# Pauses in a dispatch, a reordered prologue and two moved pieces of work in a two-layer MoE and ternary FFN kernel

## The chip, the core and the metric

One core of a Trainium2 chip runs the whole program in one launch. Its engines work side by side: TensorE (PE) multiplies, VectorE (DVE) and ScalarE (ACT) work on elements, GpSimd (POOL) does the same and issues indirect transfers, SyncE (SP) issues the plain ones. Each engine takes its own instructions strictly in order. The metric is device time in microseconds (us), from the first instruction to the last; lower is better.

## What is computed

The input x has 128 x 32 tokens of 256 numbers, 4096 rows in all. Two layers are added to it in turn. Cut to what matters, with the router's sigmoid and the quantization's clips left in words:

```python
# layer 0: a linear layer with a low-rank adapter per batch, then a mixture of experts
h = x @ W.T + scalings[idx] * ((x @ A[idx].T) @ Bm[idx].T)
scores = sigmoid(h @ gate_w.T)                    # 8 experts, the 2 best of each token
routed = sum over the two: onehot(expert) * ((silu(s*h @ w1.T) * (s*h @ w3.T)) @ w2.T)
shared = (silu(h @ ws1.T) * (h @ ws3.T)) @ ws2.T
x = x + shared + routed
# layer 1: mixing of a batch's 32 rows by a gathered 32x32 matrix, then an FFN of ternary weights
y = einsum("bct,bcd->bdt", x, cond_weights[idx1])
u = act_quant(fwht(y)) @ weight_quant(w_up).T
x = x + act_quant(fwht(relu(u) ** 2)) @ weight_quant(w_down).T
```

`weight_quant` divides by the mean absolute weight, rounds to -1, 0 or 1 and scales back. `fwht` is a Walsh-Hadamard transform.

## The kernel before

The 4096 rows are 32 tiles of 128, taken in 8 groups (`NG`) of 4 tiles (`GT`). The program has four stages.

*Projection and routing* (lines 125 to 427, in a pool named `stage`). The host has laid out transposed copies. `project(g)` makes the adapter's inner product (pa, L214), then the layer's output and the router's logits together for each tile (ph, L226 and L229); ScalarE moves them to `hc[g]`. Eight columns of the router come from a small product of W and the gate (pt_gw, L187) that VectorE copies into `WT` and `BT` (L196, L197). `route(g)` is some twenty small VectorE instructions that rank the eight scores and count, so that each token's two rows have a place `dest` in the expert's region of the buffer `xs` in device memory. Then GpSimd issues eight indirect transfers for the group (L303), one for each tile and choice: 64 in all, called the dispatch here. Every row has its own place, so that they need not wait for each other.

*Around it*: loads of all inputs on SP's queue (L141 to L160), four small ones on ScalarE's; one indirect gather of the mixing matrices (wc, L162), first in GpSimd's queue behind some memsets, which goes through device memory (cs, L168) into the block-diagonal `bd` (L181); the ternary weights, made by VectorE from `ud` (L317 to L350); a table of slots (`slot_table`, L352 to L397), which says which expert each tile of 128 dispatched rows belongs to; and zeros behind each region (`pad`, L412, on SP).

*Shared expert and slots*. `shared_up` and `shared_down` run the shared expert group by group (pt_h L435, pgs L445, hids L452, pos L460), six groups (`SHARED1`) before the slots and two after them. In the slots, SP reads 128 dispatched rows (xin, L502), TensorE turns them over (pt_s, L510), VectorE or ScalarE evacuates (xTs, L84 or L86), then come the expert's two products (pg L536, po L562), and GpSimd scatters the results (yt, L569). A first read of xin waits until the dispatch has landed; 36 pairs of slots follow each other in a pipeline. VectorE's small work for a slot is cm, c and to (L519, L525, L526).

*Combination and layer 1* (L614 to the end): adds, the mixing, the transforms and the ternary products.

The order of work on each engine is that of a scheduler which goes by what is ready in its own model, except where a call asks for program order. Tiles are tracked for dependences. Plain transfers rotate over eight semaphores, so a load also waits until the load eight before it has landed; the indirect ones do the same over eight of their own. The body of `shared_up` and `shared_down` is not changed, only its place in the file.

Of the kernel before, what the change touches and what calls it, by code (L numbers as in the profile page):

```python
# [7 lines left out]
F32 = mybir.dt.float32  # L8
# [3 lines left out]
AF = mybir.ActivationFunctionType  # L12
ALU = mybir.AluOpType
AX = mybir.AxisListType

P = 128
D = 256
B, T = 128, 32
NT = B * T // P
GT = 4  # L20
NG = NT // GT
# [14 lines left out]
SHARED1 = 6  # L36


C_ID, C_H, C_HS, C_TRI, C_E16, C_N16 = 0, 128, 256, 640, 704, 712
# [5 lines left out]
def tile_kernel(  # L45
# [20 lines left out]
    nc = tc.nc  # L66
# [9 lines left out]
    def bank(tag, name, shape=(P, 512), dtype=F32):  # L76
        return psum.tile(list(shape), dtype, tag=tag, name=name)
# [3 lines left out]
    def evac(dst, src):  # L81
        turn[0] += 1
        if turn[0] % 2:
            nc.vector.tensor_copy(dst, src)  # L84
        else:
            nc.scalar.copy(dst, src)  # L86
# [25 lines left out]
    with tc.tile_pool(name="moe", bufs=1) as moe, tc.tile_pool(name="work1", bufs=2) as work1:  # L112
# [4 lines left out]
        ws2T = ws[:, 2 * D :]  # L117
# [4 lines left out]
        tab = moe.tile([P, 2, NSLOT], I32, name="tab")  # L122


        with tc.tile_pool(name="stage", bufs=1) as stage:
            wn = stage.tile([P, 2, D], F32, name="wn")
            bn = stage.tile([P, 2, P], F32, name="bn")
# [11 lines left out]

            nc.scalar.dma_start(GW, gate)  # L140
            nc.sync.dma_start(wn, W.rearrange("(c p) d -> p c d", p=P))  # L141
            nc.scalar.dma_start(i1, idx1.rearrange("(b o) -> b o", o=1))
            nc.sync.dma_start(AT, AT_)
            nc.sync.dma_start(xT[0], xT_[0])
            nc.scalar.dma_start(
                i0, idx0.rearrange("(o b) -> o b", o=1).partition_broadcast(P)
            )
            nc.scalar.dma_start(
                sb, scal.rearrange("(o e) -> o e", o=1).partition_broadcast(P)
            )  # L150
            nc.sync.dma_start(WT[:, :, :D], WT_)
            nc.sync.dma_start(bn, Bm)
            nc.sync.dma_start(cst, consts)
            nc.sync.dma_start(BT[:, :D], BT_)
            for g in range(1, NG):
                nc.sync.dma_start(xT[g], xT_[g])
            nc.sync.dma_start(ws, shared_)
            nc.sync.dma_start(wall[:, : E * WCOL // 2], experts[:, : E * WCOL // 2])
            nc.sync.dma_start(wall[:, E * WCOL // 2 :], experts[:, E * WCOL // 2 :])
            nc.sync.dma_start(ud, updown)  # L160

            nc.gpsimd.indirect_dma_start(  # L162
                out=wc,
                out_offset=None,
                in_=cw.rearrange("s c d -> s (c d)"),
                in_offset=bass.IndirectOffsetOnAxis(ap=i1, axis=0),
            )
            nc.sync.dma_start(cs, wc)  # L168

            zeros = stage.tile([P, ROW], F32, name="zeros")  # L170
            cnt = stage.tile([P, E], F32, name="cnt")
            nc.gpsimd.memset(zeros, 0.0)
            nc.gpsimd.memset(cum[:, 0], 0.0)
# [1 line left out]
            nc.gpsimd.memset(ones, 1.0)  # L175
            nc.gpsimd.memset(half, HALF)
            nc.gpsimd.memset(bd, 0.0)
            csv = cs.rearrange("(n q) (c d) -> q c n d", q=4, d=T)
            for q in range(4):
                s = slice(32 * q, 32 * q + 32)  # L180
                nc.sync.dma_start(bd[s, :, s], csv[q])  # L181


            pt = bank("t", "pt_gw")
# [21 lines left out]
                mask, i0, cst[:, C_N16 : C_N16 + 1], scol, ALU.is_equal, ALU.mult  # L206
            )
            nc.vector.tensor_copy(upper, cst[:, C_U : C_U + P])
            nc.vector.tensor_copy(idh, ident)

            def project(g):
                pa = bank("x", f"pa{g}")
# [19 lines left out]
            def route(g):  # L232
# [66 lines left out]
                nc.vector.tensor_copy(dest, df)  # L299

                for n in range(GT):
                    for i in range(2):
                        ins = nc.gpsimd.indirect_dma_start(  # L303
                            out=xs,
                            out_offset=bass.IndirectOffsetOnAxis(
                                ap=dest[:, i, n : n + 1], axis=0
                            ),
                            in_=hc[g][:, n],
                            in_offset=None,
                        ).ins  # L310
                        tc.declare_no_dep(ins, group="xs", reason="every pair has its own row")
                        tc.add_to_no_dep_group("xs", ins)

            def ternary_weights():
                rs = stage.tile([P, 2], F32, name="rs")
                part = stage.tile([P, 2, 16], F32, name="part")
                nc.vector.tensor_reduce(  # L317
                    part,
                    ud.rearrange("p i (a b) -> p i a b", a=16),
                    AX.X,  # L320
                    ALU.add,
                    apply_absolute_value=True,
                )
                nc.vector.tensor_reduce(rs, part, AX.X, ALU.add)
                pw = bank("x", "pw", (P, 2))
                nc.tensor.matmul(pw, ones, rs, start=True, stop=True)
                wscale = stage.tile([P, 2], F32, name="wscale")
                wrec = stage.tile([P, 2], F32, name="wrec")
                nc.vector.tensor_scalar(wscale, pw, 1.0 / (FF * D), EPS, ALU.mult, ALU.max)
                nc.vector.reciprocal(wrec, wscale)  # L330

                k0 = stage.tile([P, 1], F32, name="k0")
                nc.vector.scalar_tensor_tensor(
                    k0, wscale[:, 0:1], FF**-0.5, wscale[:, 0:1], ALU.mult, ALU.mult
                )
                k1 = stage.tile([P, 2], F32, name="k1")
                nc.vector.tensor_tensor(k1[:, 0:1], k0, wscale[:, 1:2], ALU.mult)
                nc.vector.reciprocal(k1[:, 1:2], k0)  # L340
                nc.vector.tensor_scalar(k1[:, 1:2], k1[:, 1:2], EPS / QB, None, ALU.mult)
                nc.vector.tensor_copy(kc, k1.unsqueeze(2).to_broadcast([P, 2, 2]))

                outs = [upT.rearrange("p k f -> p (k f)"), dnT.rearrange("p f d -> p (f d)")]
                for i in range(2):
                    nc.vector.tensor_scalar(
                        ud[:, i], ud[:, i], wrec[:, i : i + 1], MAGIC, ALU.mult, ALU.add
                    )
                    nc.vector.tensor_scalar(ud[:, i], ud[:, i], -MAGIC, 1.0, ALU.add, ALU.min)
                    nc.vector.tensor_scalar(outs[i], ud[:, i], -1.0, None, ALU.max)  # L350
# [62 lines left out]
                    tc.declare_no_dep(ins, group="xs", reason="no pair has a row of the padding")  # L413
                    tc.add_to_no_dep_group("xs", ins)

            xg = []
            for g in range(NG):
                project(g)
                if g > 0:
                    route(g - 1)  # L420
            for g in range(NG):
                xg.append(cpool.tile([P, GT, D], F32, tag="x", name=f"x{g}", bufs=NG))
                nc.sync.dma_start(xg[g], xt[g])
            route(NG - 1)
            slot_table()
            pad()
            ternary_weights()


        def shared_up(g):  # L430
            hT = work1.tile([P, 2, GT * P], F32, tag="hT", name=f"hT{g}")
            for k in range(2):
                pt = bank("t", f"pt_h{g}_{k}")
                for n in range(GT):
                    nc.tensor.transpose(  # L435
                        pt[:, n * P : (n + 1) * P],
                        hc[g][:, n, k * P : (k + 1) * P],
                        ident,
                    )
                evac(hT[:, k], pt)  # L440
            pgs = []
            for i in range(2):
                pg = bank("m", f"pgs{g}_{i}")
                for k in range(2):
                    nc.tensor.matmul(  # L445
                        pg, ws13[:, k, i], hT[:, k], start=(k == 0), stop=(k == 1)
                    )
                pgs.append(pg)
            sil = work1.tile([P, 512], F32, tag="xa", name=f"sils{g}", bufs=4)
            hid = work1.tile([P, 512], F32, tag="xa", name=f"hids{g}", bufs=4)  # L450
            nc.scalar.activation(sil, pgs[0], AF.Silu)
            nc.vector.tensor_tensor(hid, pgs[1], sil, ALU.mult)  # L452
            return hid

        def shared_down(g, hid):
            for h in range(2):
                po = bank("o", f"pos{g}_{h}", (P, 2, D))
                for i in range(2):
                    n = 2 * h + i
                    nc.tensor.matmul(  # L460
                        po[:, i], hid[:, n * P : (n + 1) * P], ws2T, start=True, stop=True
                    )
                v = xg[g][:, 2 * h : 2 * h + 2]
                nc.vector.tensor_tensor(v, po, v, ALU.add)

        def shared(gs):
            hid = None
            for g in [*gs, None]:
                nxt = shared_up(g) if g is not None else None
                if hid is not None:  # L470
                    shared_down(*hid)
                hid = (g, nxt)

        shared(range(0, SHARED1))

        tc.no_sync_barrier()

# [402 lines left out]
```

## Time and profile before

| | |
|---|---|
| median of 13 runs | 389.69 us (386.91 to 391.38) |
| the profiled execution: its own time / its span | 390.04 us / 388.2 us |
| granted TensorE clock, mean | 0.979 |
| busy: PE / DVE / ACT / POOL | 356.3 / 223.1 / 164.2 / 227.2 us |
| share of PE in the chain that ended last | 84% |
| dispatch, L303: busy, mean of one, number | 63.8 us, 997 ns, 64 |
| scatter, L569: busy, mean of one, number | 70.0 us, 973 ns, 72 |
| transfers: mean rate over the span | 148 GB/s |

The span runs from the first to the last instruction that the profiler recorded; the time of the execution has some 1.8 us around it. Busy time is an engine's time inside instructions. TensorE is busy for 92% of the span, so most of its time is work that cannot go away; the rest is where it waited, and whose wait ended last there.

In 40 equal slices of 9.7 us, the page shows TensorE's busy share in tenths, the clock granted to it, and the transfer engines' share:

```profile
PE   3999999918997999999999999999899999999983
...
POOL 5007777787740265554655655749887887745450
PEclk9999999977999999999999999999999999999996
DMA  7999846453236354444543422155333323001111
```

The ninth slice, from 78 to 87 us, has a digit of 1 for TensorE, with a lowered clock there and in the slice after it. GpSimd's digits from the fourth to the twelfth slice are the dispatch.

### The profile page before, as it was taken

Reading aid. Unit: us, or ns where it says so; the run is one execution under the profiler, and the core shown is the slowest. Engines: PE = TensorE matmul, PEld = TensorE weight load, DVE = VectorE, ACT = ScalarE, POOL = GpSimd, SP = SyncE. Lnnn points to the kernel's source line nnn. Section 1 sums busy time; section 2 is a strip of 40 time slices with the busy share of each in tenths; the row PEclk is TensorE's granted clock in tenths of the full one; section 3 lists DMA queues with packets and bytes.
Section 4 is the critical chain, followed back from the end, with each engine's and each line's share of the span. In section 5 each row is a group of like instructions: output and inputs, shape, how many; then the busy total and the mean of one; then the engine's idle time right before and its main releaser. Section 6 shows DMA issues by size and latency. Waiting matters only on the chain.

```text
span 388.2 us, 6544 instructions
## 1 busy us (share of the span) xinstructions
PE 356.3 (92%) x2055; PEld 281.2 (72%) x2055; DVE 223.1 (57%) x714; ACT 164.2 (42%) x328; POOL 227.2 (59%) x259
## 2 busy tenths in 40 slices
PE   3999999918997999999999999999899999999983
PEld 2667767604665788887787888657789898998771
DVE  0157867794355565554655555334667576676762
ACT  1021221401111444444343444315586877777862
POOL 5007777787740265554655655749887887745450
PEclk9999999977999999999999999999999999999996
DMA  7999846453236354444543422155333323001111
GB/s 214 408 427 340 251 165 214 166 206 109 106 117 202 107 163 134 151 165 141 171 158 122 160 81 76 54 201 182 109 109 130 115 83 104 34 29 57 54 56 54
DMA packets 38882, 57.49 MB, mean 148 GB/s; under 512 B 9278, under 2 KB 28736, under 8 KB 38465
## 3 DMA queue, kind: packets, MB, share of 16 engines
q1 hardware_dynamic: 31600, 39.17, 30.5%
q0 software_dynamic: 6672, 17.84, 12.5%
q10 hardware_dynamic: 576, 0.08, 0.3%
q8 instruction: 17, 0.28, 0.3%
q14 instruction: 17, 0.13, 0.1%
HBM read 33.93 MB, written 24.18 MB: 150 GB/s over the span
## 4 chain that ended last, share of the span: by engine, by line
PE 84%; DVE 6%; DMA 2%; issue 2%; ACT 2%; POOL 2%; SPq 1%; DVEq 0%; ACTq 0%
PE pg L536 17%; PE ph L226 8%; PE po L562 8%; PE pr L722 7%; PE pf L638 7%; PE pgs L445 7%; PE pa L214 4%; PE ph L229 4%; PE pt_s L510 4%; PE py L622 4%; PE pd L760 3%; PE pu L692 3%; PE pos L460 2%; PE phd L553 2%; PE pq L750 2%
## 5 line engine op out<-in xcount | busy, mean ns | idle before, releaser
L569 POOL DMA_INDIRECT yt<-y,to x72 | 70.0, 973 | 69.3 <-DVE cm L519 24.6
L303 POOL DMA_INDIRECT xs<-hc,dest x64 | 63.8, 997 | 42.7 <-DVE s L239 23.5
L536 PE MATMUL pg<-wall,xTs 128*128 x288 | 76.7, 390 | 3.1 <-DVE cm L519 2.2
L536 PEld LDWEIGHTS pg<-wall,xTs 128*128 128x128 f32 x288 | 49.2, 190 | 15.0 <-DVE hid L545 5.4
L544 ACT ACTIVATE sil<-pg,c 128x128 f32<-128x128 f32 x72 | 26.4, 367 | 58.4 <-PE pg L536 55.5
L545 DVE SCALAR_TENSOR_TENSOR hid<-pg,c,sil 128x128 f32<-128x128 f32 x72 | 25.1, 348 | 44.5 <-ACT sil L544 44.2
L614 POOL TENSOR_TENSOR x<-x,y 128x512 f32<-128x512 f32 x32 | 40.5, 1270 | 6.4 <-PE pgs L445 5.2
L562 PE MATMUL po<-wall,hidT 128*128 x144 | 37.7, 381 | 0.0
L638 PE MATMUL pf<-cst,yT 128*128 128x256 f32 x128 | 34.9, 394 | 1.6 <-ACT yT L630 1.6
L722 PE MATMUL pr<-cst,b 128*128 128x128 f32 x256 | 34.8, 280 | 1.2 <-POOL b L711 0.7
L226 PE MATMUL ph<-WT,xT 128*128 128x264 f32 x128 | 35.5, 404 | 0.3 <-DVE WT L196 0.3
L230 ACT COPY hc<-ph 128x264 f32<-128x264 f32 x32 | 12.1, 378 | 52.2 <-PE ph L229 45.4
L722 PEld LDWEIGHTS pr<-cst,b 128*128 128x128 f32 x256 | 31.0, 192 | 1.7 <-POOL b L711 0.9
L226 PEld LDWEIGHTS ph<-WT,xT 128*128 128x128 f32 x128 | 25.5, 200 | 7.9 <-issue 2.2
L445 PE MATMUL pgs<-hT,ws 128*128 128x512 f32 x64 | 30.4, 618 | 0.4 <-DVE hT L84 0.4
L562 PEld LDWEIGHTS po<-wall,hidT 128*128 128x128 f32 x144 | 24.5, 190 | 2.2 <-ACT hidT L86 0.3
L460 PE MATMUL pos<-ws,hids 128*128 128x256 f32 x64 | 16.8, 394 | 9.0 <-DVE hids L452 9.0
L638 PEld LDWEIGHTS pf<-cst,yT 128*128 128x128 f32 x128 | 21.5, 191 | 4.3 <-ACT yT L630 2.3
L510 PE MATMUL pt_s<-cst,xin 128*128 128x128 f32 x144 | 24.2, 273 | 0.0
L736 ACT ACTIVATE q<-pr,half,sc 128x512 f16<-128x512 f32 x32 | 23.1, 779 | 2.1 <-DVE sc L733 2.1
L710 POOL TENSOR_TENSOR b<-c 128x512 f32<-128x512 f32 x16 | 20.3, 1266 | 4.2 <-DVE m L729 2.7
L445 PEld LDWEIGHTS pgs<-hT,ws 128*128 128x128 f32 x64 | 12.2, 199 | 13.9 <-issue 11.3
(137 smaller groups left out, 639.6 us busy)
## 6 DMA issues: line engine op xcount, KB each, us to landing
xin<-xs SPq DMA_DIRECT2D x72, 136.0 KB, 2.3
y<-yt SPq DMA_DIRECT2D x16, 512.0 KB, 3.7
xT<-in_xT SPq DMA_DIRECT2D x8, 512.0 KB, 8.5
x<-in_x SPq DMA_DIRECT2D x8, 512.0 KB, 4.5
out<-o SPq DMA_DIRECT2D x16, 256.0 KB, 2.1
wall<-in_experts SPq DMA_DIRECT2D x2, 1536.0 KB, 12.3
yt<-y,to POOLq DMA_INDIRECT x72, 2.6
xs<-zeros SPq DMA_DIRECT2D x8, 136.0 KB, 2.1
```

Of the source, the lines that this page charges most:

```text
L226: nc.tensor.matmul(ph, xT[g][:, k, cols], WT[:, k], start=(k == 0), stop=False)
L303: ins = nc.gpsimd.indirect_dma_start(out=xs, out_offset=bass.IndirectOffsetOnAxis(ap=dest[:, i, n : n + 1], axis=0), in_=hc[g][:, n], in_o ...
L445: nc.tensor.matmul(pg, ws13[:, k, i], hT[:, k], start=(k == 0), stop=(k == 1))
L510: nc.tensor.transpose(pt[:, i, k], xin[:, i, k * P : (k + 1) * P], ident)
L536: nc.tensor.matmul(pg[:, i].rearrange("p a f -> p (a f)"), xT[:, i, k], wall[:, bass.ds(w + k * D, D)], start=(k == 0), stop=(k == 1),)
L544: nc.scalar.activation(sil[:, i], pg[:, i, 0], AF.Silu, scale=ci)
L545: nc.vector.scalar_tensor_tensor(hid[:, i], pg[:, i, 1], ci, sil[:, i], ALU.mult, ALU.mult)
L562: nc.tensor.matmul(po[:, i], hT[:, i], wall[:, bass.ds(w + 2 * D, D)], start=True, stop=True)
L569: ins = nc.gpsimd.indirect_dma_start(out=yt, out_offset=bass.IndirectOffsetOnAxis(ap=to[:, i : i + 1], axis=0), in_=y[:, i], in_offset=Non ...
L614: nc.gpsimd.tensor_tensor(v, v, y2[:, :, r], ALU.add)
L638: nc.tensor.matmul(pf[:, i], yT[:, k, i * P : (i + 1) * P], had256[k], start=(k == 0), stop=(k == 1),)
L722: nc.tensor.matmul(pr[:, f * P : (f + 1) * P], b[:, f, i * P : (i + 1) * P], had, start=True, stop=True,)
```

## The change

Four things are edited.

1. *A pause for every eight dispatch transfers*: after each group's transfers but the last, GpSimd fills a tile `pause` of 128 x 1600 numbers that nobody reads, and the next group's transfers are issued after it.
2. *Loads in order*: `bn` goes ahead of `AT` and `xT[0]`, the constants are loaded in two parts, the second (identity and transforms) after `xT[4]`, and i1 goes last on ScalarE's queue. The f16 copy of the identity (idh) moves from the front of VectorE's work to behind the routing.
3. *The mixes' gather*, with its way through device memory into `bd`, becomes a function called after the third `project`, so that its place in GpSimd's queue is after the second pause, and cs and bd come later in SP's queue, behind four of the eight x loads.
4. *The ternary weights* are made inside the shared expert: `shared` takes a function `amid` and calls it after the third group's step. The shared functions move up in the file for that, and the call of `shared` goes inside the pool `stage`.

```diff
+            for i, g in enumerate([*gs, None]):
+                nxt = shared_up(g) if g is not None else None
+                if hid is not None:
+                    shared_down(*hid)
+                hid = (g, nxt)
+                if i == 2 and amid is not None:
+                    amid()
...
             nc.scalar.dma_start(GW, gate)
             nc.sync.dma_start(wn, W.rearrange("(c p) d -> p c d", p=P))
-            nc.scalar.dma_start(i1, idx1.rearrange("(b o) -> b o", o=1))
-            nc.sync.dma_start(AT, AT_)
-            nc.sync.dma_start(xT[0], xT_[0])
             nc.scalar.dma_start(
                 i0, idx0.rearrange("(o b) -> o b", o=1).partition_broadcast(P)
             )
+            nc.sync.dma_start(bn, Bm)
...
+            nc.sync.dma_start(AT, AT_)
+            nc.sync.dma_start(xT[0], xT_[0])
+            nc.scalar.dma_start(i1, idx1.rearrange("(b o) -> b o", o=1))
             nc.sync.dma_start(WT[:, :, :D], WT_)
-            nc.sync.dma_start(bn, Bm)
-            nc.sync.dma_start(cst, consts)
+            nc.sync.dma_start(cst[:, C_TRI:], consts[:, C_TRI:])
             nc.sync.dma_start(BT[:, :D], BT_)
             for g in range(1, NG):
                 nc.sync.dma_start(xT[g], xT_[g])
+                if g == 4:
+                    nc.sync.dma_start(cst[:, :C_TRI], consts[:, :C_TRI])
...
-            nc.gpsimd.indirect_dma_start(
-                out=wc,
-                out_offset=None,
-                in_=cw.rearrange("s c d -> s (c d)"),
-                in_offset=bass.IndirectOffsetOnAxis(ap=i1, axis=0),
-            )
-            nc.sync.dma_start(cs, wc)
...
+            pause = stage.tile([P, 1600], F32, name="pause")
...
-            nc.vector.tensor_copy(idh, ident)
...
                 for n in range(GT):
-                    for i in range(2):
-                        ins = nc.gpsimd.indirect_dma_start(
...
+                    with ExitStack() as stack:
+                        if paused:
+                            stack.enter_context(tc.issue_after(paused[-1].ins))
+                        for i in range(2):
+                            ins = nc.gpsimd.indirect_dma_start(
...
+                    if n == GT - 1 and g < NG - 1:
+
+                        paused.append(tc.keep_in_program_order(nc.gpsimd.memset(pause, 0.0)))
+
+            paused = []
...
+            def mixes():
+
+                tc.keep_in_program_order(
+                    nc.gpsimd.indirect_dma_start(
+                        out=wc,
...
+                nc.sync.dma_start(cs, wc)
+                csv = cs.rearrange("(n q) (c d) -> q c n d", q=4, d=T)
+                for q in range(4):
+                    rows = slice(32 * q, 32 * q + 32)
+                    nc.sync.dma_start(bd[rows, :, rows], csv[q])
+
             for g in range(NG):
                 project(g)
                 if g > 0:
                     route(g - 1)
+                if g == 2:
+                    mixes()
...
             route(NG - 1)
+            tc.keep_in_program_order(nc.vector.tensor_copy(idh, ident))
             slot_table()
             pad()
-            ternary_weights()
...
-        shared(range(0, SHARED1))
+            shared(range(0, SHARED1), ternary_weights)
```

More of the change, by code (lines that the diff above doesn't have):

```diff
@@ L122, in tile_kernel, with shared_up, shared_down, shared @@
         tab = moe.tile([P, 2, NSLOT], I32, name="tab")
+        xg = []
+        def shared_up(g):
+            hT = work1.tile([P, 2, GT * P], F32, tag="hT", name=f"hT{g}")
+            for k in range(2):
+                pt = bank("t", f"pt_h{g}_{k}")
+                for n in range(GT):
+                    nc.tensor.transpose(
+                        pt[:, n * P : (n + 1) * P],
+                        hc[g][:, n, k * P : (k + 1) * P],
+                        ident,
+                    )
+                evac(hT[:, k], pt)
+            pgs = []
+            for i in range(2):
+                pg = bank("m", f"pgs{g}_{i}")
+                for k in range(2):
+                    nc.tensor.matmul(
+                        pg, ws13[:, k, i], hT[:, k], start=(k == 0), stop=(k == 1)
+                    )
+                pgs.append(pg)
+            sil = work1.tile([P, 512], F32, tag="xa", name=f"sils{g}", bufs=4)
+            hid = work1.tile([P, 512], F32, tag="xa", name=f"hids{g}", bufs=4)
+            nc.scalar.activation(sil, pgs[0], AF.Silu)
+            nc.vector.tensor_tensor(hid, pgs[1], sil, ALU.mult)
+            return hid
+        def shared_down(g, hid):
+            for h in range(2):
+                po = bank("o", f"pos{g}_{h}", (P, 2, D))
+                for i in range(2):
+                    n = 2 * h + i
+                    nc.tensor.matmul(
+                        po[:, i], hid[:, n * P : (n + 1) * P], ws2T, start=True, stop=True
+                    )
+                v = xg[g][:, 2 * h : 2 * h + 2]
+                nc.vector.tensor_tensor(v, po, v, ALU.add)
+        def shared(gs, amid=None):
+            hid = None
+            for i, g in enumerate([*gs, None]):
[5 more added lines that the diff above has]
+                    amid()
         with tc.tile_pool(name="stage", bufs=1) as stage:
@@ L177, in tile_kernel @@
             nc.gpsimd.memset(bd, 0.0)
[L178 to L181, printed above, removed]
             pt = bank("t", "pt_gw")
@@ L301, in route @@
                 for n in range(GT):
-                    for i in range(2):
[L303 to L312, printed above, removed]
+                    with ExitStack() as stack:
+                        if paused:
+                            stack.enter_context(tc.issue_after(paused[-1].ins))
+                        for i in range(2):
+                            ins = nc.gpsimd.indirect_dma_start(
+                                out=xs,
+                                out_offset=bass.IndirectOffsetOnAxis(
+                                    ap=dest[:, i, n : n + 1], axis=0
+                                ),
+                                in_=hc[g][:, n],
+                                in_offset=None,
+                            ).ins
+                            tc.declare_no_dep(ins, group="xs", reason="every pair has its own row")
+                            tc.add_to_no_dep_group("xs", ins)
+                    if n == GT - 1 and g < NG - 1:
+                        paused.append(tc.keep_in_program_order(nc.gpsimd.memset(pause, 0.0)))
+            paused = []
             def ternary_weights():
@@ L414, in pad @@
                     tc.add_to_no_dep_group("xs", ins)
-            xg = []
+            def mixes():
+                tc.keep_in_program_order(
+                    nc.gpsimd.indirect_dma_start(
+                        out=wc,
+                        out_offset=None,
+                        in_=cw.rearrange("s c d -> s (c d)"),
+                        in_offset=bass.IndirectOffsetOnAxis(ap=i1, axis=0),
+                    )
+                )
+                nc.sync.dma_start(cs, wc)
[3 more added lines that the diff above has]
+                    nc.sync.dma_start(bd[rows, :, rows], csv[q])
             for g in range(NG):
@@ L424, in tile_kernel @@
             route(NG - 1)
+            tc.keep_in_program_order(nc.vector.tensor_copy(idh, ident))
             slot_table()
             pad()
-            ternary_weights()
[L430 to L472, printed above, removed]
-        shared(range(0, SHARED1))
+            shared(range(0, SHARED1), ternary_weights)
         tc.no_sync_barrier()
```

## The prediction

> **What bounds the kernel now.** I read the chain of waits first (PE 84% of it), then TensorE's timeline for the places where it stands idle, then GpSimd's, then the waits of SP's queue. TensorE is busy without a break from 13 to 71 us and from 124.5 us to the end stage, so the change can move the end only at the start or between 71 and 124.5 us. Columns of a timeline: start, duration, engine, line, what it does, and in brackets the idle time before it with its releaser.
>
> ```profile
> 8.45 3.75 PE L214 MATMUL pa<-xT,AT 128*128 128x512 f32 x4 [2.62 <-DMA xT<-in_xT]
> ...
> 88.51 1.22 PE L460 MATMUL pos<-ws,hids 128*128 128x256 f32 x2 [9.03 <-DVE hids L452]
> 89.53 4.81 PE L445 MATMUL pgs<-hT,ws 128*128 128x512 f32 x8
> ...
> 115.01 3.60 PE L445 MATMUL pgs<-hT,ws 128*128 128x512 f32 x8
> 118.45 3.00 PE L460 MATMUL pos<-ws,hids 128*128 128x256 f32 x12
> 121.28 1.04 PE L510 MATMUL pt_s<-cst,xin 128*128 128x128 f32 x8
> 124.49 1.10 PE L536 MATMUL pg<-wall,xTs 128*128 x4 [2.17 <-DVE cm L519]
> ```
>
> The reader should see two things. TensorE stands for 9.03 us before 88.51, since VectorE works off the slot table and the ternary weights before it comes to the first shared group's product (hids, L452). And the slots begin (121.28) the moment the shared groups end: their rows are already there. How nearly they were not is GpSimd's view and the SP queue's:
>
> ```profile
> 0.75 0.32 POOL L172 MEMSET zeros<- 128x272 f32 x1 [0.29 <-POOLq L867]
> ...
> 1.37 3.51 POOL L177 MEMSET bd<- 128x4096 f32 x1
> 5.04 1.12 POOL L162 DMA_INDIRECT wc<-in_cond,i  x1 [0.17 <-issue]
> 29.71 0.99 POOL L303 DMA_INDIRECT xs<-hc,dest  x1 [23.55 <-DVE s L239]
> 31.01 0.96 POOL L303 DMA_INDIRECT xs<-hc,dest  x1 [0.30 <-issue]
> ...
> 81.27 2.05 POOL L303 DMA_INDIRECT xs<-hc,dest  x1 [0.30 <-DMA xs<-hc,dest]
> ...
> 111.76 0.96 POOL L303 DMA_INDIRECT xs<-hc,dest  x1 [0.30 <-issue]
> ```
> ```profile
> 114.20 15.57 SPq L502 DMA_DIRECT2D xin<-xs  x20
> ```
> ```profile
> SPq L502 <- DMA xs<-hc,dest: 25.5, 1, 25.5
> ```
>
> GpSimd dispatches 64 transfers without a rest: 0.96 us each and 0.30 us to the next, so 1.266 us a step. From 29.71 to 111.76 are 63 steps, 82.05 us, which is 2.3 us above 63 x 1.266 (the 2.05 us one among them). The last lands at 114.20, 2.44 us after its start, and only then does SP issue the first read of a slot (L502): it had waited 25.5 us for it. The dispatch is a second path, hidden by TensorE's by little. From that first read to the first product of a slot (pg, L536) there is more than a landing: VectorE, in order, takes cm, c and to of three slots and then turns the first slot's rows over (xTs, L84):
>
> ```profile
> 123.13 0.19 DVE L519 TENSOR_TENSOR cm<-xin,oh 128x32 f32<-128x32 f32 x1
> 123.36 0.19 DVE L525 TENSOR_REDUCE c<-cm 128x4 f32<-128x32 f32 x1
> 123.58 0.17 DVE L526 TENSOR_SCALAR to<-c 128x2 int32<-128x2 f32 x1
> 123.66 0.68 DVE L84 COPY xTs<-pt_s 128x512 f32<-128x512 f32 x1
> ```
>
> The third slot's second half is SP's sixth read, issued 3.2 us after the first (117.4 against 114.20); a read lands in 2.0 to 3.3 us, 2.4 taken: 5.6 us. Then cm, c, to 0.5, xTs 0.7, and 0.15 to pg: 6.9 us after the first read, if nothing else holds it (6.0 to 7.4 by the landings). Before, that would have been 121.1: it lay just under the shared groups.
>
> **The change, part by part.**
> *Ternary weights into the shared groups* (and idh later): six VectorE instructions of 0.69 to 0.75 us and some small ones, about 5.5 us, no longer stand ahead of hids. The 9.03 us wait shrinks to what the slot table alone holds. The slow restart behind it goes too: 1.22 us for two pos matmuls where the chain elsewhere gives 0.43, and 4.61 us for eight pgs where it gives 3.43, so (1.22 - 0.43) + (4.61 - 3.43) = 1.97 us. The granted clock was 0.50 from 84 to 90 us. The shared groups would end at 121.28 - 9.03 - 1.97 = 110.3 us, plus up to 5 us of VectorE work still between them. Alone it is worth little, since the slots cannot start before 114.20 + 6.9 = 121.1, 3.4 us before today's 124.49.
>
> *Loads in order of need.* bn now precedes xT0, so the four pt_gw matmuls on it leave the path between pa and ph for the wait before pa (0.67 us, and 0.27 us for WT behind them). xT0 is issued one place later (some 0.5 us) but WT now waits for GW and the constants are cut to a third, so less competes with it; I take both together as nothing, bounds 0.5 late to 0.6 early. Gain 0.9, from 0 to 1.5 us. It moves TensorE and the dispatch's start alike. i1 goes to the end of ACT's queue; its reader is now 50 us away. The ident part of the constants comes after xT4; its first reader is the transpose at 71 us. Both at nothing; without that cover each costs one landing, 7 us.
>
> *The pauses.* Seven memsets of 128x1600 on GpSimd, each between two batches of eight: the built order shows them in that queue, every transfer behind them. Two rows give the size: (3.51 - 0.32) / (4096 - 272) = 0.834 ns an element, so 0.32 + 1328 x 0.000834 = 1.43 us. A memset is followed after 0.17 us (bd to wc) instead of 0.30, and the gap from a transfer to a memset, which no row shows, is 0 to 0.30: 1.30 to 1.60 us, 1.5 taken, 7 x 1.5 = 10.5 us (9.1 to 11.2). No row shows a memset while VectorE works; transfers kept 0.96 us with VectorE at 77%, so I take no slowing. The other end is the worst transfer, 2.05 for 0.96, 1.09 more each: 7.6 us more.
>
> *The mixes' gather* leaves 5.04 us, where GpSimd was free, for the dispatch after its second batch: 1.12 + 0.30 = 1.4 us. It landed 8.4 us after issue; the transfer that now reuses its semaphore comes 10.3 us after its start, so 0, up to 2 us if it lands later. On SP, cs waits for it (about 60 us) and four bd and four x loads queue behind. bd took 5.2 us of issue and x needs some 5 to land: by 80 us, against readers at 100 (x4) and 260 (bd). Nothing; without that cover the pads and reads behind them would slip alike.
>
> *The sum.* First slot read: 114.20 - 0.9 + 10.5 + 1.4 = 125.2 us. First pg: 132.1, against 124.49: 7.6 us later. TensorE has by then stood from about 112 to 128, so it restarts slow: 2.0 us by the row above, at the head of a stage where it is 99% busy, so nothing absorbs it. After that nothing in the program differs. 390.04 (this execution's own time) + 7.6 + 2.0 = 399.6; the median of the 13 runs is 0.35 lower, so 399.3.
>
> The Trainium skill (TensorE: Matmul & The Clock Gate, Part 1) puts the half clock at some 3.4 us of renewed work after an idle window as long, which is an estimate of 1.7 us lost instead of the 1.97 measured here, 0.3 us off the sum; it also says the loss varies with where the window falls.
>
> The Trainium skill (SBUF — State Buffer, "SBUF: two separate sides") says that a VectorE instruction in a two-port mode locks GpSimd out of writing descriptors; the 2.05 us transfer did stand beside a ternary instruction (81.06, 0.75 us). By that rule the six moved instructions still fall into the dispatch and could cost up to 6 x 0.7 = 4.2 us there, an estimate, where this trace's excess over the whole dispatch is 2.3: the sum would be 1.9 us higher. It speaks against the idea that the move relieves GpSimd.
>
> **The rivals.**
> *The pauses are free, and the gain of the ternary move shows* (faster). Were a memset to run beside the descriptors' making, the first read would be at 114.20 - 0.9 + 1.4 = 114.7 and pg at 121.6, 2.9 us earlier; TensorE would still stand from 112 to 117.7, half the restart loss, 1.0: 1.9 us gained, 388 us. It decides below 0.9 us for all seven, where 6.9 + 2.0 after the read meets 124.49. For it: nothing on GpSimd but its order. Against: memsets and the gather follow each other at the start without overlap beyond 0.06 us.
> *Pauses dearer under a busy VectorE* (slower still): 7.6 us more, 407 us. For it, the 2.05 us transfer; against, a median of 0.96 over all 64.
> *The excess of 2.3 us goes, and the start gains 1.5*: first read 120.9 with the cheapest pauses, pg 126.9 by the quickest landing, 2.4 later, and half a restart: 393.
>
> **How the numbers follow.** Forecast 0.83, its own range 394 to 403.5 (dearest: 0 gained at the start, 11.2 of pauses, 2 for the gather, 7.4 to pg: 404). Dearer pauses 0.08; free pauses 0.06; the rest, 0.03, near no change. About 0.3% is what a measurement of this kernel can tell. Faster 0.06, same 0.02, slower 0.92.
>
> **What would show it.** Right: seven memsets of about 1.4 us between the L345 batches, the first xin read near 125, a wait of TensorE above 10 us before pt_s, the hids wait mostly gone, pgs after it at 0.43 us each. Wrong: a first read before 118, or TensorE meeting the slots without a wait; or a dispatch that starts more than 2 us earlier.

## The result and the profile after

The changed kernel takes 395.68 us (median of 10 runs, 394.72 to 396.88) where the kernel before takes 389.6 (46 runs, 386.91 to 391.38): ratio 1.0167, 95% interval 1.0145 to 1.0189, so 6.1 us slower. Here and below a ratio is the measured one of the fast runs, and can differ by up to 0.2% from the quotient of the medians beside it. Its profiled execution took 395.75 us with a span of 394.0 us, against 390.04 and 388.2.

The busy shares in 40 slices, now of 9.85 us each, from the page of the changed kernel:

```profile
PE   4999899899952899999999999998899999999983
...
POOL 4028778888781055555554665649888687763550
PEclk9999999989995699999999999999999999999998
```

The weak slice at 78 to 87 us is gone; a new one stands at 108 to 128 us (digits 5 and 2), with a lowered clock in it and behind it. TensorE's timeline of the changed kernel shows both ends of what happened:

```profile
8.38 3.58 PE L253 MATMUL pa<-xT,AT 128*128 128x512 f32 x4 [1.36 <-DMA xT<-in_xT]
11.79 1.50 PE L265 MATMUL ph<-WT,xT 128*128 128x264 f32 x6
...
107.76 3.17 PE L142 MATMUL pgs<-hT,ws 128*128 128x512 f32 x7
110.76 3.00 PE L157 MATMUL pos<-ws,hids 128*128 128x256 f32 x12
124.39 0.69 PE L530 MATMUL pt_s<-cst,xin 128*128 128x128 f32 x2 [10.63 <-DMA xin<-xs]
125.43 1.73 PE L530 MATMUL pt_s<-cst,xin 128*128 128x128 f32 x6 [0.35 <-DMA xin<-xs]
129.05 2.05 PE L556 MATMUL pg<-wall,xTs 128*128 x4 [1.89 <-DVE xTs L84]
```

The shared groups end 7.5 us earlier (113.8 instead of 121.3), as the move of the ternary weights meant them to, and then TensorE stands for 10.63 us, because the dispatched rows are not there. The first pg is at 129.05, 4.56 us later than before, and its four matmuls take 2.05 us instead of 1.10. Why the rows are late is in GpSimd's timeline and SP's queue:

```profile
26.55 1.35 POOL L345 DMA_INDIRECT xs<-hc,dest  x1 [21.67 <-DVE s L278]
...
35.79 0.96 POOL L345 DMA_INDIRECT xs<-hc,dest  x1 [0.30 <-issue]
36.75 1.45 POOL L357 MEMSET pause<- 128x1600 f32 x1
38.37 0.97 POOL L345 DMA_INDIRECT xs<-hc,dest  x1 [0.17 <-ACT hc L269]
...
49.79 0.98 POOL L466 DMA_INDIRECT wc<-in_cond,i  x1 [0.16 <-DMA xs<-hc,dest]
...
119.70 0.96 POOL L345 DMA_INDIRECT xs<-hc,dest  x1 [0.30 <-issue]
```
```profile
122.14 25.41 SPq L522 DMA_DIRECT2D xin<-xs  x26
```

A memset follows a transfer without any gap (35.79 + 0.96 = 36.75) and is followed after 0.17 us: from transfer to transfer 38.37 - 35.79 = 2.58 us where 1.266 was, so 1.31 us for each pause and 9.2 for seven. The dispatch lasts 119.70 - 26.55 = 93.15 us instead of 82.05: 9.2 of pauses, 1.3 of the gather, and 2.9 us of long transfers where there were 2.3. It began 3.16 us earlier, and so the first read of a slot is at 122.14 instead of 114.20, 7.9 us later.

### The profile page after: what moved, and what is told of

It reads as the page before. It is cut to its first block, busy times and chain, and to the rows that moved or that the text cites. A ratio compares the mean times of both kernels' runs of the same rounds, so it can differ in the third digit from the quotient of the medians.

```text
span 394.0 us, 6556 instructions
## 1 busy us (share of the span) xinstructions
PE 358.1 (91%) x2055; PEld 282.1 (72%) x2055; DVE 229.6 (58%) x714; ACT 164.4 (42%) x328; POOL 237.8 (60%) x266
## 4 chain that ended last, share of the span: by engine, by line
PE 71%; POOL 7%; DVE 7%; DMA 6%; issue 4%; ACT 2%; SPq 1%; DVEq 0%; POOLq 0%; ACTq 0%
PE pg L556 17%; PE po L582 8%; PE pr L742 7%; PE pf L658 7%; PE ph L265 6%; POOL xs L345 5%; PE pt_s L530 4%; DMA xs<-hc,dest 4%; PE py L642 3%; PE ph L268 3%; PE pd L780 3%; PE pu L712 3%; PE pa L253 3%; PE phd L573 2%; PE pgs L142 2%
## 5 line engine op out<-in xcount | busy, mean ns | idle before, releaser
L556 PE MATMUL pg<-wall,xTs 128*128 x288 | 78.8, 399 | 2.8 <-DVE xTs L84 1.9
L556 PEld LDWEIGHTS pg<-wall,xTs 128*128 128x128 f32 x288 | 50.8, 195 | 14.9 <-DVE hid L565 4.6
L530 PE MATMUL pt_s<-cst,xin 128*128 128x128 f32 x144 | 26.1, 286 | 11.0 <-DMA xin<-xs 11.0
L265 PE MATMUL ph<-WT,xT 128*128 128x264 f32 x128 | 33.7, 386 | 0.0
L530 PEld LDWEIGHTS pt_s<-cst,xin 128*128 128x128 f32 x144 | 19.1, 147 | 16.2 <-DMA xin<-xs 12.1
L265 PEld LDWEIGHTS ph<-WT,xT 128*128 128x128 f32 x128 | 24.5, 191 | 7.9 <-issue 3.3
L268 PE MATMUL ph<-BT,xa 128*128 128x264 f32 x64 | 20.2, 397 | 2.2 <-DVE xa L255 2.2
```

What stands on the lines that cost most here:

```text
L265: nc.tensor.matmul(ph, xT[g][:, k, cols], WT[:, k], start=(k == 0), stop=False)
L268: nc.tensor.matmul(ph, xa[:, cols], BT, start=False, stop=True)
L530: nc.tensor.transpose(pt[:, i, k], xin[:, i, k * P : (k + 1) * P], ident)
L556: nc.tensor.matmul(pg[:, i].rearrange("p a f -> p (a f)"), xT[:, i, k], wall[:, bass.ds(w + k * D, D)], start=(k == 0), stop=(k == 1),)
```

## The experiments

The four single parts came first, then combinations. The first four runs happened to be made on another chip than the rest, and the kernel before took 424.64 us there (19 runs, 421.79 to 429.55) instead of 389.6. So every ratio is against runs of the kernel before on the same chip.

**The changed kernel without its pauses**, twice.

```
-            pause = stage.tile([P, 1600], F32, name="pause")
...
-                        paused.append(tc.keep_in_program_order(nc.gpsimd.memset(pause, 0.0)))
```

> The changed kernel without its seven pauses, all else kept. Theory (the dispatch's length sets the first read of a slot, and the slots begin 6.9 us after it): a pause lengthened the step from transfer to transfer by 1.31 us in the trace of the changed kernel, so the first read comes 9.2 us earlier, near 112.9, the first slot product near 119.8 (before: 124.49), and TensorE's wait ahead of the slots falls from 10.6 us to some 3: 385 to 387 us. Rival one (the pauses cost by holding VectorE, and through it TensorE, in the projection, 2.2 us of TensorE's waits there): 392 to 393 us. Rival two (the cost lies in the moved gather or the loads): 395 us still.

> The changed kernel without its seven pauses, a second time, beside another row of runs of the kernel before. Theory that the pauses are the loss: on a chip without stops, start 3.2 us earlier, gather 1.3 us in the row, first slot read at 112.3, first expert matmul at 119.2: 5 us less than before, ratio 0.987 (0.981 to 0.994). Rival (the gather amid the dispatch or the loads hold the row up): ratio 1.00 or more. On a chip with stops after every 16th transfer: ratio 1.00, as in the first run.

Measured: on the other chip 427.15 us, ratio 1.0044 (0.9994 to 1.0093). On the chip of all later runs, where the kernel before takes 389.4 us (16 runs), 387.92 us, ratio 0.9955 (0.993 to 0.998). There the dispatch goes from 27.85 to 111.36 us, 83.51 us, the first read is at 113.80 and pg at 120.79. The pauses are the loss: taking them out gives back 395.68 - 387.92 = 7.8 us. The gain over the kernel before, 1.5 us, is smaller than the 5 expected; pg came 1.6 us later than I had worked out (the dispatch started 1.3 us later than in the changed kernel's profile), and its matmuls run at half rate behind the wait, which the expectation left out.

**The kernel before with the pauses alone**, twice: only the memset and its order are added.

> The kernel before with the seven pauses alone. Theory: first read 9.2 us later, near 123.4, first slot product near 130.3 instead of 124.49; the shared groups still end at 121 to 124, so TensorE hardly stands and does not restart slowly: 395 to 396.5 us. Rival one (pauses cost only through VectorE): 391 to 392 us, the first slot product within 2.5 us of before's. Rival three (hidden by TensorE's own path): no change.

> The kernel before with the seven pauses alone, a second time. Theory that the pauses cost their length where nothing stops: seven times 1.31 = 9.2 us in the row of transfers, first slot read at 123.4; the shared groups end at 121.3 and so hide 2.9 us of it: 6.3 us more than before, ratio 1.016 (1.010 to 1.024). Theory that pauses let a queue drain: on a chip with stops ratio 0.97, as in the first run; there the stops are missing in the trace. Rival (the first run's gain belongs to the pauses on every chip): ratio 0.97 here too, without stops in the run of the kernel without pauses.

Measured: 396.3 us, ratio 1.018 (1.0139 to 1.0221), where the kernel before takes 389.4; on the other chip 411.92 us against 424.64, ratio 0.9697 (0.9619 to 0.9774). The pauses cost 6.9 us on the one chip and gain 12.7 on the other. On the first, the dispatch lasts 118.72 - 27.24 = 91.48 us, 9.4 us longer, and the shared groups, which end at 122.8 there, cover part of it.

On the other chip something holds up several engines. GpSimd's timeline of the changed kernel without pauses has three stops there, each behind 16 transfers (the first also behind the gather):

```profile
47.32 0.97 POOL L462 DMA_INDIRECT wc<-in_cond,i  x1 [0.30 <-issue]
52.53 1.12 POOL L344 DMA_INDIRECT xs<-hc,dest  x1 [4.23 <-issue]
...
77.17 1.06 POOL L344 DMA_INDIRECT xs<-hc,dest  x1 [4.55 <-ACT s L275]
...
102.40 1.13 POOL L344 DMA_INDIRECT xs<-hc,dest  x1 [4.83 <-ACT hT L86]
```

The releasers named are no explanation: "issue" means that the profile shows nothing to wait for. The same stops (4.1 to 5.5 us, again three) stand in both other kernels without pauses on that chip; in the kernel with pauses there is none, nor in any kernel on the chip of the later runs. The other engines wait too. This is ScalarE's timeline of the same kernel on the same chip:

```profile
38.20 0.38 ACT L268 COPY hc<-ph 128x264 f32<-128x264 f32 x1 [2.05 <-PE ph L267]
43.86 0.38 ACT L268 COPY hc<-ph 128x264 f32<-128x264 f32 x1 [5.28 <-remote]
49.50 0.38 ACT L268 COPY hc<-ph 128x264 f32<-128x264 f32 x1 [5.27 <-remote]
```

and VectorE's:

```profile
50.19 0.19 DVE L323 TENSOR_TENSOR row<-pp,cst 128x32 f32<-128x32 f32 x1 [10.48 <-remote]
```

Each waits for TensorE alone, whose products of that group (ph, pp) the trace has finished by 39.3 us. "Remote" means a release that the profile ties to no instruction. ScalarE's first long wait begins at 38.6 us, almost 10 us before GpSimd first stops (52.53 - 4.23 = 48.30), so that stop does not cause it.

Nor do the stops set the time there. The first read of a slot is issued at 127.31 us in this kernel, but TensorE comes to the slots only at 149.87, when its shared groups end, and finds the rows there:

```profile
147.03 3.00 PE L157 MATMUL pos<-ws,hids 128*128 128x256 f32 x12
149.87 1.04 PE L526 MATMUL pt_s<-cst,xin 128*128 128x128 f32 x8
153.07 1.10 PE L552 MATMUL pg<-wall,xTs 128*128 x4 [2.17 <-DVE cm L535]
```

In the kernel before with the pauses alone, on the same chip, the same lines come 12.6 us earlier, about as much as the time gained:

```profile
134.46 3.00 PE L469 MATMUL pos<-ws,hids 128*128 128x256 f32 x12
137.29 1.04 PE L519 MATMUL pt_s<-cst,xin 128*128 128x128 f32 x8
140.49 1.10 PE L545 MATMUL pg<-wall,xTs 128*128 x4 [2.17 <-DVE cm L528]
```

(The kernel before itself has no profile on that chip. With the new loads alone, which took the same time there, pg is at 153.09.) Without pauses TensorE has three waits of 7.1 to 9.7 us for VectorE's xa and ScalarE's hc around the projections; with them, the longest there is 3.81. The waits don't all go: ScalarE still has a remote one of 6.35 us before 96.86, though GpSimd never stops. So on that chip a break after every eight transfers takes away GpSimd's stops and shortens the waits of the engines beside it, and the time was gained by the second. What causes the stops and the waits, and why only there, no run shows; nor was the whole changed kernel run on that chip.

**Half the pause**: `pause = stage.tile([P, 800], ...)` in the changed kernel.

> The changed kernel with pauses of 128x800 instead of 128x1600. Theory that each pause costs its own length less the 0.13 us of gap that it takes the place of: 0.73 - 0.13 = 0.60 us each, 4.2 us in all instead of 9.2: 5 us less than the changed kernel, some 390.5 where the kernel before takes 389.6, ratio 1.002 (0.996 to 1.008). Rival (a pause has a fixed price, whatever its length): ratio 1.017 as for the changed kernel. On a chip with stops: if the pause's length counts, between 0.97 and 1.00 with stops left over in the trace; if any break is enough, 0.97 or less.

Measured: 391.74 us, ratio 1.0063 (1.0036 to 1.0089). It is 3.8 us above the kernel without pauses and 3.9 below the changed kernel: the price goes with the length. The dispatch lasts 116.26 - 28.25 = 88.01 us, 4.5 more than without pauses, 0.64 each.

**The ternary weights amid the shared groups, alone**, twice.

```
-            ternary_weights()
...
-        shared(range(0, SHARED1))
+            shared(range(0, SHARED1), ternary_weights)
```

> The kernel before with the ternary weights moved into the shared groups alone. Theory: TensorE's wait of 9.03 us before the first pos goes and the shared groups end near 112, but the first read stays at 114.2 and the first slot product comes 6.9 us after it, near 121.1: 3.4 us earlier than before, less up to 1.2 us for a slow restart: 386.5 to 388 us. Rival (TensorE's path alone counts): the whole 9.03 + 1.97 us, 379 us.

> The kernel before with the ternary weights moved amid the shared groups, alone, a second time. Theory: VectorE's 10 us of ternary work no longer stand ahead of the shared groups, these end some 7.5 us earlier, and the first expert matmul follows the first slot read by 7.0 to 7.5 us (10.3 before): 2.5 to 3 us less than before, ratio 0.993 (0.989 to 0.997) on a chip without stops. Rival (the ternary work amid the groups delays them as much as it did ahead of them): the wait between the two stays 10 us, ratio 1.00. On a chip with stops after every 16th transfer: 1.01, as in the first run.

Measured: 388.06 us against 389.3 (30 runs of the kernel before), ratio 0.995 (0.9918 to 0.9983); on the other chip 429.45, ratio 1.0106 (1.0025 to 1.0186). TensorE's timeline of the second of the two:

```profile
109.00 3.00 PE L157 MATMUL pos<-ws,hids 128*128 128x256 f32 x12
117.47 1.31 PE L513 MATMUL pt_s<-cst,xin 128*128 128x128 f32 x4 [5.48 <-DMA xin<-xs]
```

The shared groups end at 112.0 us although this execution started its dispatch late (30.62). The wait for VectorE has become a wait of 5.48 us for the rows: the dispatch, second by little before, is now first. pg follows the first read (115.22) at 122.34, 7.1 us, as expected.

**The order of loads alone**, twice: the hunk of the loads from the change, and nothing else.

> The kernel before with the new order of loads and the later idh copy alone. Theory: the three us by which the changed kernel's second projection began earlier (17.14 against 20.40) come from TensorE's clock, raised at 11.8 instead of 17.4 us, since the small products on bn now fill the wait before xT0; nothing takes them back here, so the dispatch begins near 26.6, the shared groups end near 118, the first slot product near 121.3: 386 to 387 us. Rival (only the moved products count, as the prediction had it): 0.9 us, 388.8 us. Rival (the time is taken back by 71 us, as in the changed kernel, where the projections ended only 0.5 us earlier): 389.2 us.

> The kernel before with the new order of loads alone, a second time. In the ten profiles so far the dispatch begins at 27.2 to 29.7 us (mean 28.3) with the old order and at 26.2 to 28.3 us (mean 27.1) with the new. Theory (TensorE's shared groups, not the slot read, set the first expert matmul while the ternary weights stand ahead of them): the start's 1.1 us reach the end only as far as the projections and the shared groups come earlier too: ratio 0.997 to 1.001. Rival (the 3.2 us of the first two profiles are the loads' work): ratio 0.992.

Measured: 388.44 us, ratio 0.9969 (0.9941 to 0.9998), 0.9 us less than before and not the 2.6 to 3.6 of the first theory; on the other chip 424.81, ratio 1.0017 (0.9981 to 1.0053). In this profile the dispatch starts at 28.11, 1.6 us earlier than in the first profile of the kernel before, but pg at 124.17 only 0.3 earlier: the 9 us wait for hids and the shared groups behind it set pg here, not the dispatch.

**The kernel before, once more**, for a second profile.

> The kernel before, unchanged, for a second profile of it. Theory: the beginning of the dispatch at 29.7 us in the first profile was late by the moment at which the first matmuls fall to half their length, which differs from execution to execution; here it is 27 to 29 us. Rival (29.7 belongs to the order of loads): 29.4 to 30.0 again. Ratio 1.00 by both.

Measured: 389.05 us, ratio 0.9987 (0.995 to 1.0025), and a dispatch that starts at 29.86 us. My expectation of 27 to 29 failed, and the rival's number came. But the rival doesn't hold either: with the old order of loads the six profiles have 27.24, 27.76, 28.37, 29.71, 29.86 and 30.62 (mean 28.9), with the new order eight have 26.21 to 28.25 (mean 27.2). The new order gains some 1.8 us on average (standard error 0.6), and a single pair of these profiles can show from 1 us lost to 4.4 gained.

**Loads and ternary weights together**, with the gather at the front and no pauses.

> The kernel before with the new order of loads and the ternary weights amid the shared groups; the gather stays at the front, no pauses. Theory (the path is the GpSimd's row of transfers): on a chip where the transfers go out one behind the other at 1.266 us, the dispatch begins 3.2 us earlier and loses nothing, the first slot read comes at 114.2 - 3.2 = 111.0 us, the first expert matmul 6.9 us behind it at 118, 6.5 us before that of the kernel before: 6 us less than before, ratio 0.985 (0.979 to 0.992). Rival (TensorE's shared groups set the first expert matmul and stay where they were): ratio 1.00. On a chip where GpSimd stops 4 to 5 us after every 16th transfer, as in the first four runs: ratio 0.99 to 1.01, the start's gain is spent in the stops.

Measured: 385.89 us (5 runs, 384.93 to 386.24) against 389.4, ratio 0.992 (0.9891 to 0.9948). It is the fastest version found: 3.5 us below the kernel before, 9.8 below the changed one. From TensorE's timeline:

```profile
113.22 0.69 PE L520 MATMUL pt_s<-cst,xin 128*128 128x128 f32 x2 [4.23 <-DMA xin<-xs]
...
118.12 2.04 PE L546 MATMUL pg<-wall,xTs 128*128 x4 [1.97 <-DVE cm L529]
```

The first read (110.94) and pg (118.12) are where they were expected; the time gained less than pg's 6.4 us and than the 6 expected. In the profile 1.0 of that is given back behind pg, where the matmuls restart at half rate (2.04 us for four); the rest, between a profile of 384.93 us and a median of 385.89, against 390.04 and 389.4, is the spread of single executions. The two parts alone gave 0.9 and 1.2 us, together 3.5: each alone leaves the other path standing, as their traces show (the intervals are too wide for the times alone to show it). Against this kernel, the one without pauses differs only by the gather's place: 387.92 - 385.89 = 2.0 us for moving it into the dispatch, of which its step in the queue is 1.28.

**Seven shared groups ahead of the slots** in that fastest version: `SHARED1 = 7`.

> The kernel with the loads and the ternary weights (no pauses, gather at the front) and with seven shared groups ahead of the experts instead of six. Theory: the seventh group (5.9 us) fills the 4.2 us in which TensorE waits for the first slots, and the matmuls behind that wait no longer take twice their length (1.2 us): 0.99 of the kernel before, or 1 us less than with six groups, if the last group's absence at 248 to 254 us leaves no wait there. Rival: TensorE then stands idle ahead of the mixing, where the same 6 us covered the wait for the rows of the results, and nothing is gained or 1 us lost: ratio 0.992 to 0.996.

Measured: 389.1 us, ratio 0.9985 (0.9955 to 1.0016): worse than with six groups by 3.2 us, more than the rival had allowed. The seventh group does fill the wait for the rows (from 4.23 to 0.4 us), and pg still runs at half rate (2.04 us at 118.19). But at the other end TensorE has nothing to do while it waits for the experts' results:

```profile
248.65 1.99 PE L157 MATMUL pos<-ws,hids 128*128 128x256 f32 x8 [0.85 <-DVE hids L149]
257.13 2.08 PE L632 MATMUL py<-bd,x 128*128 128x128 f32 x8 [6.49 <-POOL x L624]
```

The mixing starts at 257.13 instead of 255.25, and at half rate: py takes 2.08 us for its eight instead of 1.16. The work was moved from one cover to another that was worth more.

## Why the prediction was right, and where its numbers were off

It said slower, 399.3 us with 394 to 403.5, by pauses that lengthen the dispatch until it outlasts the shared groups. The runs show that mechanism; the number is 3.6 us high. By its steps:

- *The pauses*, 10.5 us by 1.5 each: 1.31 each in the trace, 9.2. The gap ahead of a memset, put at 0 to 0.30, was 0. Over the whole dispatch the difference is 9.4 to 9.6 us, 1.35 to 1.38 a pause. The length is confirmed by halving it.
- *The gather*, 1.4 us: 1.28 us for its step in the queue, 2.0 in the time.
- *The excess of long transfers*, left at 2.3: it was 2.9 in this trace, and 1.5 to 2.6 in the other kernels on this chip, the pauses and the gather taken off.
- *The start*, 0.9 us with 0 to 1.5: this is the step that was most off. It was 3.16 in the two profiles, beyond both its bound and the 2 us that the prediction named as a sign of error. In the kernel before, the matmuls keep taking about twice their length until some 17 us (ph at 13.12, ten in 4.33 us), in the changed one only until 11.8 (six in 1.50 us). How far they do differs from execution to execution: with the old order those ten ph took 2.49 us in three profiles and 4.33 to 4.66 in three. Some 1.8 us is the mean gain over fourteen profiles, and the rest of the 3.16 belongs to this pair. That the loads alone gained 0.9 us in time, the figure worked out from the small matmuls, is a coincidence: the 0.9 was meant for the start, which came 1.6 earlier in that profile. The profile's granted clock reads 1.00 from 13 to 17 us in both kernels. What ends the slow start, and whether the earlier small matmuls bring it forward, stays open.
- *First read*: 125.2 predicted, 122.14 measured. The difference of 3.1 is 2.3 of start, 1.3 of pauses, 0.1 of the gather, less 0.6 of excess.
- *Read to pg*, 6.9 us: 129.05 - 122.14 = 6.9.
- *The slow restart*, 2.0: from pg to the end of the span are 264.95 us, and 263.71 before, so 1.2 in this pair. Leaving out the other chip and the kernel with seven groups, the mean over the six kernels that waited for the rows is 265.2 (264.6 to 266.1), over the three profiles without such a wait 263.5 (262.7 to 264.2): 1.6. The estimate of 1.7 that was worked out from the Trainium skill (TensorE: Matmul & The Clock Gate, Part 1) lies nearer to both than the 2.0 of the sum. With the first read's 3.1, the 0.8 by which this term was too large makes up the 3.9 between 399.6 and the 395.75 of the profiled execution.
- *The ternary weights*: the wait for hids is gone, as said, and alone the move gains 1.2 us of the 3.4 that the prediction allowed it. The slow restart behind that wait, which was to go too, went in the kernels with the move that have no pauses or half of them (3.60 us for eight pgs). In the changed kernel eight take 4.74 at 81.04, at a mean granted clock of 0.72 from 78 to 84 us, so the sign "pgs after it at 0.43 each" did not come. It costs nothing here, as the rows are later still. The 1.9 us that the rule of the Trainium skill (SBUF — State Buffer, "SBUF: two separate sides") would have added did not come either: in the three kernels on this chip with the move, the gather in front and no pauses, the 63 steps took 81.27, 82.16 and 82.32 us, against 82.05 and 82.08 before. As the ternary work falls into the dispatch in all five, they don't test the rule itself.

One step left half of the question out: "no row shows a memset while VectorE works; I take no slowing". The memset is not slowed (1.45 or 1.46 us for all seven), but VectorE is, by the memset. Its timeline in the changed kernel, beside the first pause:

```profile
36.09 2.15 DVE L297 TENSOR_SCALAR chosen<-rank 128x32 bf16<-128x32 f32 x1
36.18 2.06 DVE L299 SCALAR_TENSOR_TENSOR hc<-rank,s 128x32 f32<-128x32 f32 x1
36.28 1.96 DVE L303 TENSOR_TENSOR to<-rank,cst 128x32 f32<-128x32 f32 x1
38.27 0.16 DVE L314 TENSOR_TENSOR before<-before,chosen 128x8 bf16<-128x8 bf16 x1
```

All three end when the memset does, at 38.2. The first that is held is a TENSOR_SCALAR at each of the four pauses that fall on such work, and those behind it wait in order; a SCALAR_TENSOR_TENSOR inside the second memset (48.20) kept its length. The mean of L297 by group of instructions went from 222 ns without pauses to 708 ns (564 with half the pause). TensorE waited 2.2 us for VectorE's xa in the projections because of it, which the prediction has not: the projections end at 71 us, only 0.5 earlier than before for a start 3.16 earlier. The shared groups still end before the rows come, so it costs nothing here. The Trainium skill (SBUF — State Buffer, "SBUF: two separate sides") states this side as well: of a VectorE instruction in a two-port mode and a GpSimd instruction, the one that starts first keeps the shared ports for its whole length, and the other waits. I had read only the half in which VectorE comes first. The trace agrees on the wait. It doesn't show an instruction's mode, nor who came first: L297 is recorded from 36.09, before the memset (36.75), inside the last transfer ahead of it.

The whole account in times: loads and ternary weights -3.5 us, the gather's place +2.0, the pauses +7.8, together +6.3. These are steps of one row of kernels, so they must add up to the changed kernel's 6.1; the 0.2 is the difference between two medians of the kernel before. What they show is the size of each.

## What to carry over

Two paths that end some 3 us apart are read as two bounds: shortening the one that is first (the ternary work) is worth only the distance to the second, and lengthening the second (the dispatch) costs all but that distance. A pause in a queue is paid at its length wherever nothing stops that queue; before adding one, look in the trace of the chip at hand for the waits that it is to prevent, and for whether they lie on the path that sets the time, for here it costs 1.8% on one chip and gains 3% on another. And a step at the very start of a kernel should be read from several profiles: here a single pair gave 3.2 us where the mean is 1.8.

## What the runs showed of the hardware

- The same kernel took 389.4 and 424.6 us on two chips. On the second, GpSimd stops for 4.1 to 5.5 us after every 16 indirect transfers issued in a row, and ScalarE and VectorE have waits of 5 to 11.5 us, some of which begin before a stop. With a memset of 1.45 us after every eight there is no such stop, and the longest remote wait of the two in the dispatch is 6.35 us. Cause not known.
- A memset on GpSimd starts without a gap behind an indirect transfer (0 instead of 0.30 us) and holds up a small VectorE TENSOR_SCALAR, and what is queued behind it, until it ends (2.15 us for one of 0.18).
- A wait of TensorE for the rows is followed by matmuls of twice the length, 2.04 us for four instead of 1.10, even where it waited only 0.5 to 0.7 us at a time for rows and then 2.5 for VectorE, as in the kernel before with the pauses alone; the granted clock was 0.50 there from 128 to 134 us. The kernel before, which only had 2.17 us of waiting ahead of pg, kept a clock of 1.00.
